# Two edits to a written order of work: a new list for one stretch, and four boundary columns moved

## The chip, the cores and the metric

The kernel runs on one core of a Trainium2 chip. Time is device time in microseconds (us), from the start of the program to its end; lower is better. Five engines work side by side, each taking its own instructions strictly in order: TensorE (PE, matmuls and transposes), VectorE (DVE), ScalarE (ACT), GpSimd (POOL) and SyncE (SP), which issues all DMA transfers. They wait for each other through semaphores. SBUF is the on-chip memory, PSUM the banks that PE writes to.

## The reference, cut to what matters

Input is x, 4 images of 256 x 256 positions with 64 channels, in 32-bit floats. Layer 0:

```python
h  = pw(layernorm(x, g1, b1), w_te, b_te)            # 64 -> 128 channels
F  = fft2(h)                                         # over the two image axes
fc = gelu(pw(concat(real(F), imag(F)), w_fc, b_fc))  # 256 -> 256 channels
sp = real(ifft2(re(fc) + 1j * im(fc)))
x1 = x + pw(sp, w_tp, b_tp)                          # 128 -> 64
h2 = pw(layernorm(x1, g2, b2), w_fe, b_fe)           # 64 -> 128
d  = gelu(depthwise_conv3x3(h2, w_dw) + b_dw)
x2 = x1 + pw(d, w_fp, b_fp)                          # 128 -> 64
```

Layer 1 takes x2 as a sequence along the first image axis, subtracts a moving average of 25, applies a complex matrix to each channel's first 128 frequencies, goes back and adds the average. The kernel makes one 256 x 256 matrix per channel of all this.

## The kernel before, in words

All Fourier transforms are matmuls with tables of sines and cosines, and symmetries halve them. Work comes in four kinds of units:

- **Forward chunks** (128 of them, 32 to an image): load a chunk of x ("fl"), its statistics ("fq" squares on ACT, line 327; "fr" sum on DVE, line 330; "fR", "fm" sum of squares, line 337; "fM" variance, line 341; "fp" power of -1/2 on POOL, line 347), scale it ("fx", POOL, line 354), then fold it by symmetry into halves ("fa", DVE, line 391), quarters ("fb", DVE, line 411) and halves again ("fh0", "fh1", POOL, line 416), transform along one axis ("y0", "y1", PE, line 422), evict ("yt0", "yt1", ACT, line 440) and store to DRAM. "fa" and "fh" write a tile xb that exists once; y0 and y1 read it. The squares go to a tile "sq" that also exists once and is shared by all statistics.
- **Pairs** of frequency columns (65 pairs to an image, two per period): transform along the other axis ("x", PE, line 527), evict ("xs", ACT, line 542), mix channels in two halves ("m0", "m1", PE, line 551), evict one part ("gc0", "gc1", ACT, line 565), add and subtract the other ("b0", "b1", DVE, line 570), gelu ("g0", "g1", ACT, line 574), fold ("p0", "p1", POOL, line 580), project ("z", PE, line 604), evict ("zs", ACT, line 612), transpose ("w", PE, line 621), evict ("zt", ACT, line 631).
- **Back steps**, one per period: transform back ("u", PE, line 653), evict ("us", ACT, line 670), combine ("uc", DVE, lines 683 and 684; "uf", DVE, lines 702 and 715) and store to DRAM.
- **Convolution chunks** (128, 32 to an image): load ("ul", "xl"), finish the first column ("c0", line 771), transform back along the first axis ("s", PE, line 813), add to x ("r0", "r1", DVE, lines 826 and 833), statistics of the same six kinds ("cq", "cr", "cR", "cm", "cM", "cp"), scale ("cx"), to channels ("t", "tt"), row sums ("T", POOL, lines 870 to 875), products ("gm", "gh", "em", "eh", PE, lines 896 and 915), evict and combine ("gc_", "cf", "ce", lines 935 to 947), edges ("cE"), gelu ("a", line 964), project ("o", PE, line 971), turn ("ft", PE, line 992), add and store ("st", line 1006).

Three frequency columns of each image that have no mirror partner among the stored ones are made apart, by "cc" (`other_columns`, line 773), once for each image, for its first chunk. It allocates the shared tile, loads two pieces into it, makes nine small DVE instructions on it and stores the result to DRAM; later chunks load it:

```python
v = shared.tile([P, 8, 2, C], F32, tag="sq", name=f"fix_{b}")
for i in range(2):
    nc.sync.dma_start(v[:, 2 * i : 2 * i + 2], u_ds[b][i][:, :, 0])   # line 781
...                                                # lines 784 to 796, DVE
nc.sync.dma_start(fixed[b], v[:, 3:6])             # line 797
```

The order is written out by hand. Program order is what the functions are called in, and each engine gets its instructions in that order; SP's alone are placed by the framework. The loop over periods n runs through a list of operations; each entry names an operation and an offset, and `do` first runs whatever the operation depends on by the table FOLLOWS:

```python
def period(n):
    for op, at in FULL if any(n - k in chunk_at for k in range(5)) else SPECTRUM:
        n0 = 2 * (n - S0) if op in PAIRS else n - S0 if op in BACK else n
        do(op, n0 + at)
```

For n below 35 a loop of its own (`starting`) does forward chunks beside layer 1's matrices. From n = 35 to 70 the list is SPECTRUM: forward chunks, pairs and back steps of the first image, and no convolution yet. From n = 71 on it is FULL, with convolution chunks. "cc" acts in the periods n = 71, 104, 136 and 169, the first convolution chunk of each image. Forward chunks end with n = 128, so the last two have none beside them. After the last period, layer 1 is applied in a stage of its own (line 1153), whose first inputs are loaded (lines 1133 and 1140) before the fourth image's chunks.

[...] a matmul into a bank waits for the last reader of what was there.

Of the kernel before, what the change touches and what calls it, by code (L numbers as in the profile page):

```python
# [129 lines left out]
def conv_seq_kernel(ctx: ExitStack, tc: tile.TileContext, a: dict, tables: bass.AP, out: bass.AP):  # L130
    nc = tc.nc
    x = a["x"]
# [11 lines left out]
    def column(ap):  # L144
        return ap.rearrange("(p o) -> p o", o=1)
# [46 lines left out]
    with tc.tile_pool(name="prep", bufs=1) as prep:  # L192

        def load(shape, name, src):
            t = prep.tile(shape, F32, tag=name, name=name)
            nc.sync.dma_start(t, src)
            return t

        w_te = load([C, HID], "w_te", a["w_te"])
        g1 = load([C, 1], "g1", column(a["g1"]))  # L200
        b1 = load([C, 1], "b1", column(a["b1"]))
# [1008 lines left out]
    def numbered(text):  # L1210

        return [(w.split(":")[0], int(w.split(":")[1]) if ":" in w else 0) for w in text.split()]

    follows = {}
    for line in FOLLOWS.replace("\n", "|").split("|"):
# [4 lines left out]

    FULL = numbered("""
        c0 s cf0:-3 cf1:-3 b0:-1 b1:-1 r0 r1 fx:-1 g0:-1 z:-2 zs:-2 x xs g1:-1 p0:-1 p1:-1
        o0:-4 fs0:-4 o1:-4 fs1:-4 ul:1 cq cr cR cm cM cp t0:-1 tt0:-1 t1:-1 tt1:-1 w:-2 zt:-2
        cx em:-3 eh:-3 T1:-1 T0:-1 fq fr fR fm fM fp m0 gc0 m1 gc1 ce0:-3 ce1:-3 cE:-3
        u us b0 b1 uc z:-1 zs:-1 x:1 xs:1 y0:-2 y1:-2 yt0:-2 yt1:-2 fl:1 a0:-3 a1:-3
        fa:-1 fb:-1 fh0:-1 fh1:-1 ft0:-4 ft1:-4 st0:-4 st1:-4 xl:1 cc w:-1 zt:-1 uf
        g0 g1 p0 p1 gm:-2 gh:-2 gc_0:-2 gc_1:-2 m0:1 gc0:1 m1:1 gc1:1 UL:1 XL:1
    """)

    SPECTRUM = numbered("""  # L1230
        fl:1 p0:-2 fq x z:-2 fr g0:-1 b1:-1 y0:-2 fx:-1 zs:-2 w:-2 fm xs g1:-1 m0 yt1:-2 zt:-2 fa:-1
        m1 u gc1 fR gc0 p0:-1 yt0:-2 fb:-1 us b1 fM p1:-1 b0 x:1 g1 fh1:-1 z:-1 fh0:-1 xs:1 m0:1
        zs:-1 uc gc0:1 w:-1 uf g0 m1:1 zt:-1 b0:1 fp y1:-1 gc1:1 p1
        UL:1 XL:1
    """)
    PAIRS = set("x xs m0 m1 gc0 gc1 b0 b1 g0 g1 p0 p1 z zs w zt".split())
# [119 lines left out]
```

## Time and profile before

| | |
|---|---|
| runs | 4531.76, 4535.45 and 4537.56 us (median 4535.45) |
| the profiled execution | 4535.69 us, span 4533.9 us |
| busy, share of the span | PE 96%, DVE 79%, POOL 61%, ACT 55% |
| chain that ended last | PE 75%, DVE 9%, POOL 4%, DMA 2%, issue 2% |

The profile is of one execution. Busy times are per engine; a group is all instructions of one line and shape, with total busy time, the mean of one in nanoseconds, and the idle time of the engine just before them. In the order of time, a line gives the start, the length, the engine, the source line, the operation, what it writes and reads, how many instructions were merged, and in brackets how long the engine had been idle and what released it. The clock column is TensorE's granted clock as a share of the full one.

### The profile page before, as it was taken

Reading aid. Unit: us, or ns where it says so; the run is one execution under the profiler, and the core shown is the slowest. Engines: PE = TensorE matmul, PEld = TensorE weight load, DVE = VectorE, ACT = ScalarE, POOL = GpSimd, SP = SyncE. Lnnn points to the kernel's source line nnn. Section 1 sums busy time; section 2 is a strip of 40 time slices with the busy share of each in tenths; the row PEclk is TensorE's granted clock in tenths of the full one; section 3 lists DMA queues with packets and bytes.
Section 4 is the critical chain, followed back from the end, with each engine's and each line's share of the span. In section 5 each row is a group of like instructions: output and inputs, shape, how many; then the busy total and the mean of one; then the engine's idle time right before and its main releaser. Section 6 shows DMA issues by size and latency. Waiting matters only on the chain.

```text
span 4533.9 us, 63718 instructions
## 1 busy us (share of the span) xinstructions
PE 4352.5 (96%) x22347; PEld 2231.7 (49%) x22347; DVE 3596.7 (79%) x5451; ACT 2505.2 (55%) x3686; POOL 2775.2 (61%) x1806
## 2 busy tenths in 40 slices
PE   7998888889999999999999999999999899999999
PEld 4543333345555555455555555555555455554444
DVE  6778999989999999999999777777777788862222
ACT  2337888666666666666666666666664344431111
POOL 5887888787888877788777555555554555530000
PEclk9999999999999999999999999999999999999999
DMA  5665555434444444444443333333334332329998
GB/s 171 203 191 153 141 143 149 136 107 131 131 130 131 134 130 133 125 134 135 136 137 119 93 117 98 98 105 97 105 105 131 111 103 93 102 78 321 324 331 268
DMA packets 764775, 655.02 MB, mean 144 GB/s; under 512 B 40141, under 2 KB 649375, under 8 KB 764328
## 3 DMA queue, kind: packets, MB, share of 16 engines
q1 hardware_dynamic: 764456, 650.95, 47.6%
q8 instruction: 179, 2.93, 0.3%
q14 instruction: 140, 1.15, 0.1%
HBM read 364.81 MB, written 286.00 MB: 144 GB/s over the span
## 4 chain that ended last, share of the span: by engine, by line
PE 75%; DVE 9%; POOL 4%; issue 2%; DMA 2%; SPq 0%; ACT 0%; POOLq 0%; DVEq 0%; ACTq 0%
PE ps_h_c L896 19%; PE ps_h_c L915 11%; PE ps_o L1153 8%; PE ps_p L551 7%; PE ps_f_c L971 5%; PE ps_s_c L813 5%; PE ps_z L604 4%; PE ps_u L653 4%; PE ps_x L527 4%; PE ps_t_c L850 3%; PE ps_ft_c L992 3%; DVE xb L391 2%; PE ps_y L422 2%; PE ps_zt L621 2%; DVE g L570 2%
## 5 line engine op out<-in xcount | busy, mean ns | idle before, releaser
L580 POOL TENSOR_TENSOR g<-g 128x512 f32<-128x512 f32 (+1 forms) x520 | 709.8, 1375 | 514.1 <-ACT g L574 514.0
L896 PE MATMUL ps_h_c<-td_c,wc_main 128*128 128x512 f32 x2048 | 923.9, 594 | 8.8 <-DVE h_c L941 8.8
L570 DVE TENSOR_TENSOR g<-ps_p,g 128x512 f32<-128x512 f32 x1040 | 693.6, 682 | 28.5 <-ACT g L565 10.4
L574 ACT ACTIVATE g<-g,b_fc 128x1024 f32<-128x1024 f32 (+1 forms) x520 | 585.7, 1146 | 225.7 <-DVE g L570 225.6
L347 POOL TENSOR_TENSOR rstd_c<-var_c,minus_half 128x16 f32<-128x16 f32 x128 | 371.8, 2905 | 478.7 <-DVE var_c L341 470.1
L551 PE MATMUL ps_p<-xs,wp 64*128 64x512 f32 (+1 forms) x2080 | 513.5, 604 | 63.9 <-ACT xs L542 61.7
L565 ACT COPY g<-ps_p 128x512 f32<-128x512 f32 (+1 forms) x520 | 299.1, 584 | 478.4 <-PE ps_p L551 476.4
L896 PEld LDWEIGHTS ps_h_c<-td_c,wc_main 128*128 128x128 f32 x2048 | 370.0, 191 | 379.1 <-issue 302.8
L915 PEld LDWEIGHTS ps_h_c<-td_c,wc_half 64*128 64x128 f32 x4032 | 418.0, 187 | 244.4 <-issue 195.0
L915 PE MATMUL ps_h_c<-td_c,wc_half 64*128 64x128 f32 (+1 forms) x4032 | 516.1, 393 | 3.9 <-POOL td_c L870 3.9
L1153 PE MATMUL ps_o<-xc,mt 128*128 128x512 f32 x1024 | 446.5, 598 | 15.7 <-DMA xc<-x_d 15.7
L347 POOL TENSOR_TENSOR rstd<-var,minus_half 128x16 f32<-128x16 f32 x128 | 373.0, 2914 | 82.0 <-DVE var L341 45.6
L416 POOL TENSOR_TENSOR xb<-xt 128x512 f32<-128x512 f32 x256 | 324.8, 1289 | 158.3 <-DVE xt L411 156.3
L947 DVE TENSOR_TENSOR h_c<-h_c,ps_h_c 128x512 f32<-128x512 f32 x512 | 317.4, 683 | 127.8 <-PE ps_h_c L915 127.7
L964 ACT ACTIVATE h_c<-h_c,b_conv 128x1024 f32<-128x1024 f32 x256 | 280.3, 1145 | 199.7 <-DVE h_c L960 199.7
L1167 DVE TENSOR_SCALAR oc<-ps_o,b_fp 128x512 f32<-128x512 f32 x128 | 96.1, 751 | 363.9 <-PE ps_o L1153 335.9
L940 DVE TENSOR_TENSOR h_c<-h_c,ps_h_c 128x512 f32<-128x512 f32 x256 | 175.8, 687 | 196.4 <-PE ps_h_c L915 192.8
L1153 PEld LDWEIGHTS ps_o<-xc,mt 128*128 128x128 f32 x1024 | 195.9, 192 | 265.6 <-issue 237.8
L527 PEld LDWEIGHTS ps_x<-tab,yb 128*64 128x64 f32 x4064 | 248.7, 139 | 146.6 <-issue 125.4
L604 PE MATMUL ps_z<-g,w_tp 128*64 128x512 f32 x1024 | 281.1, 610 | 38.9 <-POOL g L580 35.5
L551 PEld LDWEIGHTS ps_p<-xs,wp 64*128 64x128 f32 x2080 | 199.4, 188 | 212.8 <-issue 108.4
L1165 ACT ACTIVATE oc<-ps_o,b_fp 128x512 f32<-128x512 f32 x128 | 87.9, 687 | 375.5 <-PE ps_o L1153 326.8
(137 smaller groups left out, 7781.2 us busy)
## 6 DMA issues: line engine op xcount, KB each, us to landing
y_d<-yt SPq DMA_DIRECT2D x256, 256.0 KB, 2.6
yb<-y_d SPq DMA_DIRECT2D x256, 256.0 KB, 3.8
x_c<-in_x_dram SPq DMA_DIRECT2D x128, 512.0 KB, 5.3
u_d<-ut SPq DMA_DIRECT2D x256, 256.0 KB, 4.0
x_d<-st SPq DMA_DIRECT2D x128, 512.0 KB, 3.6
xc<-x_d SPq DMA_DIRECT2D x64, 1024.0 KB, 7.7
out_dram<-oc SPq DMA_DIRECT2D x256, 256.0 KB, 4.0
xt<-in_x_dram SPq DMA_DIRECT2D x504, 128.0 KB, 2.6
```

What stands on the lines that cost most here:

```text
L347: nc.gpsimd.tensor_tensor(rstd, var, minus_half.to_broadcast([P, n]), ALU.pow)
L416: nc.gpsimd.tensor_tensor(sums[j][:, i], x0, x1, (ALU.add, ALU.subtract)[i])
L527: nc.tensor.matmul(ps[r * C : (r + 1) * C, j * N + t * P : j * N + (t + 1) * P], blk[:, t, k, r * C : (r + 1) * C], tb[:, t, :], start=Tru ...
L551: nc.tensor.matmul(ps[:, :nf], wp[rows, cols], rhs[rows], start=True, stop=r == 1 or not pr["special"],)
L570: nc.vector.tensor_tensor(gt[:, i], re, gt[:, 1], op)
L574: nc.scalar.activation(g, g, AF.Gelu, bias=b_fc[:, half : half + 1])
L580: nc.gpsimd.tensor_tensor(g[:, 0], g[:, 0], g[:, 1], op)
L604: nc.tensor.matmul(ps[r * C : (r + 1) * C, :nf], w_tp, d[:, :nf], start=True, stop=True)
L896: nc.tensor.matmul(ps, wc_main[:, par, k, :], ts[(*j, k)].rearrange("p j i -> p (j i)"), start=True, stop=False,)
L915: nc.tensor.matmul(pss[k, par][:, s * P : (s + n) * P], wc_half[lo : lo + C, k, :], ts[(*at_q, k)][lo : lo + C, at : at + n, :].rearrange( ...
L947: nc.vector.tensor_tensor(g, g, m, (ALU.add, ALU.subtract)[r])
L1153: nc.tensor.matmul(ps[:, :nf], mts[i // CM][:, i % CM, t, to * P : (to + 1) * P], xc[:, t, :, :, i, :], start=t == 0, stop=t == 1,)
```

## The change

SPECTRUM is replaced by another order of the same operations with other offsets, and in FULL the entry "cc" moves from near the end of the list to just behind the statistics of the chunk, between "cM" and "cp". No operation is added or removed, except for what the offsets leave over from one period to the next.

```diff
     FULL = numbered("""
         c0 s cf0:-3 cf1:-3 b0:-1 b1:-1 r0 r1 fx:-1 g0:-1 z:-2 zs:-2 x xs g1:-1 p0:-1 p1:-1
-        o0:-4 fs0:-4 o1:-4 fs1:-4 ul:1 cq cr cR cm cM cp t0:-1 tt0:-1 t1:-1 tt1:-1 w:-2 zt:-2
+        o0:-4 fs0:-4 o1:-4 fs1:-4 ul:1 cq cr cR cm cM cc cp t0:-1 tt0:-1 t1:-1 tt1:-1 w:-2 zt:-2
         cx em:-3 eh:-3 T1:-1 T0:-1 fq fr fR fm fM fp m0 gc0 m1 gc1 ce0:-3 ce1:-3 cE:-3
         u us b0 b1 uc z:-1 zs:-1 x:1 xs:1 y0:-2 y1:-2 yt0:-2 yt1:-2 fl:1 a0:-3 a1:-3
-        fa:-1 fb:-1 fh0:-1 fh1:-1 ft0:-4 ft1:-4 st0:-4 st1:-4 xl:1 cc w:-1 zt:-1 uf
+        fa:-1 fb:-1 fh0:-1 fh1:-1 ft0:-4 ft1:-4 st0:-4 st1:-4 xl:1 w:-1 zt:-1 uf
         g0 g1 p0 p1 gm:-2 gh:-2 gc_0:-2 gc_1:-2 m0:1 gc0:1 m1:1 gc1:1 UL:1 XL:1
     """)
 
     SPECTRUM = numbered("""
-        fl:1 p0:-2 fq x z:-2 fr g0:-1 b1:-1 y0:-2 fx:-1 zs:-2 w:-2 fm xs g1:-1 m0 yt1:-2 zt:-2 fa:-1
-        m1 u gc1 fR gc0 p0:-1 yt0:-2 fb:-1 us b1 fM p1:-1 b0 x:1 g1 fh1:-1 z:-1 fh0:-1 xs:1 m0:1
-        zs:-1 uc gc0:1 w:-1 uf g0 m1:1 zt:-1 b0:1 fp y1:-1 gc1:1 p1
+        fr m0:-1 x g1:-1 xs p1:-1 gc0:-1 x:1 fq m0 z:-2 b0:-1 y1:-2 xs:1 fm gc0 m1 fR zs:-2 g0:-1
+        gc1 w:-2 fx:-1 fl:1 y0:-2 fM zt:-2 b0 p0:-1 fp z:-1 fa:-1 fb:-1 yt1:-2 fh1:-1 u b1 yt0:-2
+        zs:-1 us fh0:-1 uc m1:1 w:-1 g0 gc1:1 b1:1 p0 zt:-1 g1 p1 uf
         UL:1 XL:1
     """)
```

## The prediction

> **What bounds the kernel now.** I read the stretches first (busy time of each engine in windows that I cut at the stages), then the groups, the order in time and the waits inside them. Columns after the window: its length, then busy us and instructions of PE, PE weight loads, DVE, ACT and POOL.
>
> ```profile
> 416.00:823.00 407.00, 351.11 (x2208) 149.22 (x2208) 401.47 (x528) 328.48 (x498) 340.29 (x221) 1.00 0.52 145
> ...
> 1040.00:2484.00 1444.00, 1435.70 (x8222) 754.97 (x8220) 1365.60 (x2074) 956.06 (x1396) 1135.61 (x722) 1.00 0.44 132
> ...
> 2484.00:3423.00 939.00, 939.00 (x5468) 507.82 (x5466) 725.72 (x1170) 589.83 (x867) 500.54 (x361) 1.00 0.34 101
> ```
>
> 416 to 823 is the stretch without convolution (the list SPECTRUM): DVE is busy 401.5 of 407 us and PE 351.1, so DVE sets the pace. In the other two (the list FULL) PE is busy for 1435.7 of 1444 and all of 939 us: there each PE stall is lost time. In the order in time, line 683 returns every 14.68 us in the first stretch: 28 such periods and some irregular ones at both ends make up the list's 36. FULL's period is 27.73 us, later 26.01. DVE's groups in 416 to 823 (count | busy us, mean ns | idle before):
>
> ```profile
> L570 DVE TENSOR_TENSOR g<-ps_p,g 128x512 f32<-128x512 f32 x221 | 151.7, 686 | 3.9
> ...
> L391 DVE TENSOR_TENSOR xb<-xt 128x512 f32<-128x512 f32 x54 | 86.7, 1644 | 1.2
> ...
> L411 DVE TENSOR_TENSOR xt<-xb 128x512 f32<-128x512 f32 (+1 forms) x54 | 34.4, 678 | 0.0
> ```
>
> Lines 391 and 411 do the same arithmetic on the same size, but 391 takes 1644 ns and 411 678. The order in time (start, length) shows why:
>
> ```profile
> 511.10 1.29 POOL L580 TENSOR_TENSOR g<-g 128x512 f32<-128x512 f32 x1
> ...
> 511.41 3.21 DVE L391 TENSOR_TENSOR xb<-xt 128x512 f32<-128x512 f32 x2
> ...
> 512.74 1.33 POOL L580 TENSOR_TENSOR g<-g 128x512 f32<-128x512 f32 x1 [0.34 <-ACT g L574]
> ...
> 514.65 1.29 DVE L411 TENSOR_TENSOR xt<-xb 128x512 f32<-128x512 f32 x2
> ```
>
> Each of the two line-391 instructions ends only after a POOL addition. So of DVE's 14.68 us, 3.13 go to line 391 (start 511.41 to the next start 514.54) where line 411 needs 1.21: DVE's own sum is 14.68 - 1.9 = 12.8 us. PE needs 351.1/407 x 14.68 = 12.7, POOL 12.3, ACT 11.8. No list can do much better than 12.8.
>
> The second edit concerns "cc", nine small DVE instructions, four times in all. First time, in FULL's first period:
>
> ```profile
> 899.73 1.35 DVE L786 TENSOR_TENSOR fix<-fix 128x128 f32<-128x128 f32 x1
> ...
> 902.16 2.58 POOL L580 TENSOR_TENSOR g<-g 128x512 f32<-128x512 f32 x2
> ...
> 902.27 1.34 DVE L789 TENSOR_TENSOR fix<-fix 128x128 f32<-128x128 f32 x1
> ...
> 908.31 1.15 ACT L574 ACTIVATE g<-g,b_fc 128x1024 f32<-128x1024 f32 x1 [9.96 <-DVE g L570]
> ```
>
> They take 899.3 to 906.9, 7.6 us, stretched by POOL in the same way; ACT sits idle 9.96 us. The third time they take 1.8 us, with their loads issued 11 us ahead:
>
> ```profile
> 2675.31 1.23 SPq L781 DMA_DIRECT2D fix<-u_d  x2
> ...
> 2686.30 0.26 DVE L784 TENSOR_TENSOR fix<-fix 128x128 f32<-128x128 f32 x1
> ```
>
> The fourth waits for its loads, which SP issues behind four 1 MB loads of the last stage:
>
> ```profile
> 3496.03 13.50 SPq L1133 DMA_DIRECT2D xc<-x_d  x4
> ...
> 3513.66 2.66 SPq L781 DMA_DIRECT2D fix<-u_d  x2
> ...
> 3520.14 0.29 DVE L784 TENSOR_TENSOR fix<-fix 128x128 f32<-128x128 f32 x1 [14.52 <-DMA fix<-u_d]
> ...
> 3523.41 3.78 PE L896 MATMUL ps_h_c<-td_c,wc_main 128*128 128x512 f32 x4 [8.79 <-DVE h_c L941]
> ```
>
> Landing times in the DMA view (last column, us), and what PE does after a stall:
>
> ```profile
> fix<-u_d SPq DMA_DIRECT2D x8, 128.0 KB, 2.6
> ...
> fix_d<-fix SPq DMA_DIRECT2D x4, 192.0 KB, 3.1
> ...
> 1819.70 1.98 PE L604 MATMUL ps_z<-g,w_tp 128*64 128x512 f32 x4 [3.40 <-DVE h_c L941]
> ```
>
> Line 604 x4 takes 1.03 us at 1802.41 but 1.98 after the second cc's 3.40 us stall; the clock of 1816 to 1830 is 0.76.
>
> **What the Trainium skill says.** "SBUF — State Buffer", section "Who interferes with whom": a VectorE instruction with two SBUF inputs and a GpSimd instruction that reads SBUF exclude each other for a whole instruction. The trace agrees (1644 against 678 ns); lines 570 (one input in PSUM) and 330 (one input) keep 686 and 1208 ns beside POOL, and line 715 (two inputs) ran its 1.23 us at 505.31 under POOL's line 347, so that one hardly locks. "DMA: Bandwidth & Descriptors", section "Anatomy of one DMA — SWDGE (gpsimd) path": about 2 us of a DMA are fixed, mostly the receipt, and waiting is done on the issuing sequencer. Here 2.6 and 3.1 us. "TensorE: Matmul & The Clock Gate", section "What's actually happening": after about 3.4 us idle the clock halves. Agrees with the last line above.
>
> **The change, part 1: the list.** It adds and removes no instruction; it changes who queues behind whom. DVE's cycle becomes: fr, b0 of the odd pair, fm, fR, fM, b0 of the even pair, fa, fb, b1 even, uc, b1 odd, uf. Now fa, line 391, comes after POOL's p0 and beside its line 347 (fp), which hardly locks, so most of the 1.9 us goes. But new waits come. The longest loop of hand-overs, from the program's order, its buffers and banks, and the start-to-start times of the trace at 500 to 530, starting at ACT's xs (even) = 0:
> - m0 on PE after xs: 0.62 (503.68 to 504.30). PE in order: m0 1.06, z 0.90, y1 0.94, m1 1.03, w 0.59, then y0 at 5.14.
> - fa writes the only xb buffer, which y0 reads: from y0's start to DVE 1.15 (1002.43 to 1003.58): fa at 6.29. DVE, which ended b0 at 5.3, idles 1.0. POOL's p0 frees the port at about 6.3 too.
> - fa 1.30, fb 1.21, b1 even 1.33, uc 1.31: b1 odd at 11.44; the gelu g1 odd 1.45 later (501.18 to 502.63) at 12.89; it takes 1.05, then the next xs: 13.94.
>
> A second loop is as long: z even frees g for gc0 (1.15), zs and g0 follow on ACT (0.48 each), p0 1.24 later, then on POOL p0 1.3, fp 2.87, fh 2.52, p0 1.27, then uf holds the port 1.22, p1 1.35 to the next z: 13.9. Two loops at 13.9 that touch each other, with some twenty hand-overs: I take 14.1, between 13.9 and 14.7. At about 30 periods that is 30 x (14.68 - 14.1) = 17 us gained. At the seam to FULL the new list leaves one m, gc and y undone that the old had done: +2. Fill at the front: unknown, 0 ± 4.
>
> **Part 2: cc behind the statistics.** Line 780's tile is the one "sq" buffer. Before, cc's loads start after fm and DVE reaches the nine instructions at the period's end. Now they start after cm and DVE stands at them at once; behind them queue fr, fm, then cf_rest (947) or b (570); and fq on ACT waits until the result has left "sq" (line 797).
> - DVE: two loads, the second issued 0.65 after the first, land 2.6 later: 3.4 us. POOL's xn (354, 1.9 us) is running then (at 1800.28 in the second case), so the first instruction waits until about +5.0; then 1.9 us, since POOL waits for fM: +6.9.
> - First and second time: the store lands 2.6 after cc, fq 1.06, fm 1.2, fM: +12.2 where it was +2.6: 9.6 us late for everything behind, and on ACT gc, so PE's u and z stand about 8 us.
> - First time, outside the PE-bound part: before, the 7.6 us there; after, 9.6 earlier. fh, p and z come 10 late, the statistics of the next chunk 5: I take +4.
> - Second: PE stands 8 us and then runs 3 slow; before, it lost 4.1 (five periods from 1787.7 took 142.8 for 138.7). Less 1 of cover: +6.
> - Third: no forward chunk left, so no fq; but POOL's four td instructions (1.04 each) follow xn and let through one cc instruction each: cc ends near +10.9, line 947 8.5 late (2677.7 before), u waits for it 7.5 us, and the clock costs about 2; before, cc cost nothing (chunks at 26.01 on). +9.
> - Fourth: the loads stay behind the four big ones (until 3509.5) and land near 3516 to 3518; DVE now waits from 3501, with line 947 behind it, where before that ran at 3501.06. PE stops near 3504.5 until about 3519.5 and needs 10 us to where it stood at 3514.6: 3529.5 against 3523.4, some made good after: +5.
>
> Sum: +24 (12 to 34). If PE had work queued ahead of each wait it would be nothing; in FULL PE has no slack, so I take nothing off but what is said.
>
> **Sum.** -17 + 2 + 24 = +9 on the profiled execution's 4535.7 (span 4533.9, 1.8 around it), which is at the median of the runs, 4535.45: 4545. What counts as a change here is 0.2%, 9 us.
>
> **Rivals.**
> 1. *The list reaches DVE's floor and wins.* Place: the wait of fa for y0. If y0 came 1 us sooner (z not waiting for p1, m0 earlier), the period would be 12.9 to 13.3: 30 x 1.55 = 46 gained, -46 + 2 + 24 = -20: 4516. For: DVE's sum of 12.8. Against: the second loop at 13.9. It decides for faster below about 13.5 us a period.
> 2. *The list is no faster*: uf and p1 meet in the wrong order at the shared port, or hand-overs add 0.05 each, and the period is 14.6 or more. Nothing gained, +24 to +45: 4565. For: 14.68 has no hand-over on its path, since DVE never waits, while the new loops consist of them.
> 3. *cc is absorbed*: fix lands before POOL's xn starts, fq's wait is covered, each costs 1 to 3 us. Then -17 + 2 + 8 = -7, no change: 4529. For: in the FULL stretch before 2484 DVE has 5% free. Against: PE has none.
>
> **How the numbers follow.** As worked (net 0 to +20): 0.45, of which 0.17 under +9. Rival 2: 0.22. Rival 1: 0.16. Rival 3: 0.17, of which 0.03 beyond -9. So faster 0.19, same 0.31, slower 0.50. The likeliest case alone: 4536 to 4556. For 8 in 10, a tenth is left below (half of rival 1's cases) and a tenth above: 4519 to 4572.
>
> **What would show it.** Line 683's spacing near 14.1 (rival 1: 13.3; rival 2: 14.6 and over); line 391's mean down from 1644 to under 800 ns; DVE idle about 1 us before 391, released by PE's ps_y. DVE idle before line 784 released by DMA, 3 to 5 us three times and about 15 the fourth; ACT's line 327 waiting for the store of line 797; PE stalls of 7 to 9 us near the second and third cc. Past each cc the periods of 27.73, 26.01 and 16.37 should return unchanged. I am wrong if PE does not stall at cc or the new period is off by over 0.5.

## The result and the profile after

The changed kernel takes 4539.15 us (median of 6 runs, 4535.04 to 4542.61), the kernel before 4532.73 (6 runs, three of them those of the table above, 4528.77 to 4537.56): a ratio of 1.0012, interval 0.9999 to 1.0025. That is +6.4 us, inside the 9 us (0.2%) that the prediction took as no change; the interval just reaches below 1, so that these runs alone do not settle even its sign. Forecast were 4545, in a range of 4519 to 4572.

One caution for reading the traces. The profiled execution of the changed kernel took 4535.04 us and lies at the low end of its runs; that of before took 4535.69 and lies 3 us above its median. The pair of traces differs by -0.6 us in all, the medians by +6.4. So I read differences inside a stretch from the traces, and totals from the medians.

Behind the nearly unchanged time stand two opposite effects of over 20 us. First the stretches of the changed kernel, as shown for before (window: its length, then busy us and instructions of PE, PE weight loads, DVE, ACT, POOL, then the clock). I end the first window 23 us earlier, since the stretch ends earlier:

```profile
416.00:800.00 384.00, 356.70 (x2168) 142.61 (x2166) 363.08 (x524) 322.62 (x490) 359.74 (x218) 0.99 0.54 151
1040.00:2484.00 1444.00, 1431.48 (x8196) 752.12 (x8194) 1359.01 (x2065) 953.20 (x1392) 1131.08 (x717) 1.00 0.44 131
2484.00:3423.00 939.00, 933.39 (x5411) 504.06 (x5408) 724.00 (x1158) 587.77 (x862) 494.72 (x358) 1.00 0.34 100
```

In the stretch without convolution DVE is now busy 363.1 of 384 us; before, it was busy 401.5 of 407. In the two PE-bound windows PE is busy 4.2 and 5.6 us less than before: the second and the third cc lie in them.

DVE's groups of the first window (count | busy us, mean ns | idle before):

```profile
L570 DVE TENSOR_TENSOR g<-ps_p,g 128x512 f32<-128x512 f32 x218 | 149.4, 686 | 3.8
L391 DVE TENSOR_TENSOR xb<-xt 128x512 f32<-128x512 f32 x54 | 34.9, 688 | 13.8 <-PE ps_y L422 13.8
L411 DVE TENSOR_TENSOR xt<-xb 128x512 f32<-128x512 f32 (+1 forms) x54 | 34.4, 678 | 0.9
```

Line 391 fell from 1644 to 688 ns, which is line 411's speed: it no longer meets POOL's folds. In their place stands a wait for y0, 13.8 us in 27 times. One period in order of time:

```profile
512.33 0.56 ACT L542 COPY xs<-ps_x 128x512 f32<-128x512 f32 x1
...
517.31 1.28 POOL L580 TENSOR_TENSOR g<-g 128x512 f32<-128x512 f32 x1 [0.69 <-ACT g L574]
...
517.52 1.08 PE L422 MATMUL ps_y<-xb,tab 128*64 128x512 f32 x4
...
518.54 2.91 POOL L347 TENSOR_TENSOR rstd<-var,minus_half 128x16 f32<-128x16 f32 x1
...
518.71 1.29 DVE L391 TENSOR_TENSOR xb<-xt 128x512 f32<-128x512 f32 x2 [0.52 <-PE ps_y L422]
...
523.77 1.41 DVE L570 TENSOR_TENSOR g<-ps_p,g 128x512 f32<-128x512 f32 x2
...
526.27 0.56 ACT L542 COPY xs<-ps_x 128x512 f32<-128x512 f32 x1
```

From xs (line 542) to the xs of the next period it is 13.94 us. The prediction had y0 at 5.14 after xs (here 517.52 - 512.33 = 5.19), fa at 6.29 (6.38), b of the odd pair at 11.44 (11.44) and the next xs at 13.94 (13.94).

Now the first cc, in the same view:

```profile
866.41 1.23 SPq L781 DMA_DIRECT2D fix<-u_d  x2
...
869.59 0.29 DVE L784 TENSOR_TENSOR fix<-fix 128x128 f32<-128x128 f32 x1 [3.00 <-DMA fix<-u_d]
869.65 1.99 POOL L354 TENSOR_TENSOR xn_c<-x_c,rstd_c 128x1024 f32<-128x1024 f32 x1
869.80 1.99 DVE L785 TENSOR_TENSOR fix<-fix 128x128 f32<-128x128 f32 x1
...
873.20 0.34 SPq L797 DMA_DIRECT2D fix_d<-fix  x1
...
875.35 1.06 ACT L327 ACTIVATE sq<-xt 128x1024 f32<-128x1024 f32 x1 [10.07 <-DVE var L334]
...
876.93 3.68 PE L422 MATMUL ps_y<-xb,tab 128*64 128x512 f32 x8 [8.38 <-ACT g L565]
```

DVE stands 3.0 us for the loads, then a second time under POOL's line 354. ACT's line 327 begins 2.15 us after the store of line 797 was issued. The view names DVE's line 334 as its releaser, but that instruction had been done for 0.8 us (it began at 874.34 and took 0.18): what it really waited for was the shared tile "sq", which the store was still reading (a later run, below, names the store). Behind line 327 ACT's evictions queue, and PE idles 8.38 us. The second cc goes the same way:

```profile
1787.50 1.06 ACT L327 ACTIVATE sq<-xt 128x1024 f32<-128x1024 f32 x1 [9.77 <-DVE var L334]
...
1789.08 3.68 PE L653 MATMUL ps_u<-zt,tab 128*64 128x512 f32 x8 [7.16 <-ACT g L565]
```

The third cc, where line 354 and then the row sums (lines 870 to 875) run on POOL, and the clock of the window around it (the last number but two):

```profile
2663.56 0.29 DVE L784 TENSOR_TENSOR fix<-fix 128x128 f32<-128x128 f32 x1 [3.01 <-DMA fix<-u_d]
...
2665.68 1.12 DVE L786 TENSOR_TENSOR fix<-fix 128x128 f32<-128x128 f32 x1
...
2666.62 1.08 POOL L871 TENSOR_TENSOR td_c<-tt 128x512 f32<-128x512 f32 x1
...
2670.20 2.47 DVE L947 TENSOR_TENSOR h_c<-h_c,ps_h_c 128x512 f32<-128x512 f32 x4
...
2670.93 3.68 PE L653 MATMUL ps_u<-zt,tab 128*64 128x512 f32 x8 [5.61 <-DVE h_c L947]
...
2674.40 1.92 PE L604 MATMUL ps_z<-g,w_tp 128*64 128x512 f32 x4
```

```profile
2668.00:2680.00 12.00, 9.07 (x43) 4.65 (x44) 10.40 (x21) 3.54 (x5) 1.79 (x2) 0.72 0.14 43
```

The nine instructions take from 2663.56 to 2670.2. PE waits 5.61 us, and afterwards a line-653 and a line-604 group take 3.68 and 1.92 us, where they took 1.89 and 1.08 elsewhere in this trace: the clock is 0.72 in that window. The fourth stands behind the large loads as before, but now line 947 has to wait behind it too, and PE idles 15.83 us where it idled 8.79:

```profile
3489.76 13.67 SPq L1133 DMA_DIRECT2D xc<-x_d  x4
...
3503.53 4.14 SPq L781 DMA_DIRECT2D fix<-u_d  x2
...
3511.66 0.29 DVE L784 TENSOR_TENSOR fix<-fix 128x128 f32<-128x128 f32 x1 [16.96 <-DMA fix<-u_d]
...
3514.19 3.78 PE L896 MATMUL ps_h_c<-td_c,wc_main 128*128 128x512 f32 x4 [15.83 <-DVE h_c L947]
```

And what the tile of cc shows in total: DVE waited for its loads four times, where before it did once (14.5 us).

```profile
  DVE fix L784: 25.9, 4
...
DMA to landing us min/median/max: 1.9/2.5/7.7
```

### The profile page after: what moved, and what is told of

It reads as the page before. It is cut to its first block, busy times and chain, and to the rows that moved or that the text cites. A ratio compares the mean times of both kernels' runs of the same rounds, so it can differ in the third digit from the quotient of the medians.

```text
span 4533.3 us, 63491 instructions
## 1 busy us (share of the span) xinstructions
PE 4365.8 (96%) x22347; PEld 2223.1 (49%) x22347; DVE 3557.2 (78%) x5451; ACT 2505.6 (55%) x3686; POOL 2802.9 (62%) x1806
## 4 chain that ended last, share of the span: by engine, by line
PE 80%; POOL 7%; issue 4%; DVE 3%; DMA 3%; ACT 2%; SPq 0%; POOLq 0%; ACTq 0%; DVEq 0%
PE ps_h_c L896 19%; PE ps_h_c L915 11%; PE ps_o L1153 8%; PE ps_p L551 8%; PE ps_z L604 5%; PE ps_f_c L971 5%; PE ps_s_c L813 4%; PE ps_u L653 4%; PE ps_x L527 4%; PE ps_y L422 3%; POOL xb L416 3%; PE ps_ft_c L992 3%; PE ps_t_c L850 3%; POOL rstd L347 2%; PE ps_zt L621 2%
## 5 line engine op out<-in xcount | busy, mean ns | idle before, releaser
L580 POOL TENSOR_TENSOR g<-g 128x512 f32<-128x512 f32 (+1 forms) x520 | 737.2, 1430 | 531.6 <-ACT g L574 531.5
```

Of the source, the lines that this page charges most:

```text
L580: nc.gpsimd.tensor_tensor(g[:, 0], g[:, 0], g[:, 1], op)
```

## The experiments

To see where each kernel gains or loses, I set the start of the same instruction in its trace against that in the trace of before: line 683 up to the second image's cc, line 826 (convolution) after it. Negative is earlier than before. The step from one column to the next is what that place costs. (In the kernels that give cc a tile of its own, the line numbers from 784 on are 8 or 9 higher: the nine instructions begin at line 793, the store is line 805, and line 826 is line 834.)

| kernel | first line 683 | end of the stretch | past 1st cc | past 2nd | past 3rd | past 4th | median us |
|---|---|---|---|---|---|---|---|
| changed kernel | -4.1 | -25.3 | -18.5 | -14.9 | -6.3 | +0.3 | 4539.15 |
| new list alone | -4.2 | -25.4 | -23.7 | -25.8 | -25.8 | -25.8 | 4511.46 |
| cc moved alone | +5.6 | +3.9 | +9.0 | +12.7 | +21.5 | +29.8 | 4559.51 |
| own tile | -2.1 | -23.2 | -23.0 | -27.5 | -27.5 | -19.6 | 4516.38 (1 run) |
| loads ahead | -2.8 | -23.9 | -23.8 | -28.2 | -28.2 | -34.9 | 4502.02 |
| loads ahead, old place | -1.7 | -22.7 | -20.9 | -23.0 | -23.0 | -29.2 | 4505.97 |
| loads ahead, large loads later | -3.2 | -24.3 | -24.2 | -28.7 | -28.7 | -40.2 | 4495.09 |

The first column scatters by some 10 us: the kernel with cc moved alone, whose program up to there is that of before, stands at +5.6. Single executions differ by that much ahead of the stretch, so whether the new list also gains a few microseconds in its fill cannot be read here, and the readings below start from the first column.

**The two parts alone.** The new list with cc in its old place:

```diff
-        ... ul:1 cq cr cR cm cM cc cp t0:-1 ...        (FULL of the changed kernel)
+        ... ul:1 cq cr cR cm cM cp t0:-1 ...
-        ... st0:-4 st1:-4 xl:1 w:-1 zt:-1 uf
+        ... st0:-4 st1:-4 xl:1 cc w:-1 zt:-1 uf
```

> The new list alone, cc in its old place. Theory (the list gains about 25 us by the end of its stretch, and cc behind the statistics gives the same sum back): about 4533 - 24 = 4509, 4504 to 4514, ratio near 0.995; line 683 every 13.94 us in the stretch, the first cc as before (7.6 us on DVE beside POOL's folds). Rival (the lead made in the stretch cannot be kept, because the start of FULL waits for something else, so that cc's cost in the changed kernel is only the loss of that lead): between 4527 and 4533, and the lead of line 683 gone within the first five FULL periods.

Measured: 4511.46 us (before 4531.20), ratio 0.9955 (0.9942 to 0.9967): -19.7 us. The stretch gains 21.2 us in its 31 periods (-4.2 to -25.4). The seam to FULL takes 1.7 of it back, 2.1 more come at the second place, and the lead is kept to the end. The rival, that the lead is lost anyway, falls.

The other part, cc behind the statistics with the old SPECTRUM:

> cc behind the statistics alone, with the old list. Theory (cc costs +7, +3.5, +8.7 and +6.5 at its four places, whatever the list): about 4533 + 25 = 4558, 4552 to 4564, ratio near 1.0055; line 683 every 14.68 us in the stretch. Rival (the cost of the first cc is the price of the new list's seam, or the four overlap with the list's gain): 4533 + 15 to 19, about 4550, with the first cc costing 0 to 2.

Measured: 4559.51 us, ratio 1.0059 (1.0045 to 1.0073): +28.3 us. From the end of the stretch on, the four places cost 5.1, 3.7, 8.8 and 8.3, together 25.9; in the changed kernel they cost 6.8 (1.7 of it the list's seam), 3.6, 8.6 and 6.6. The first of these was expected at 7, which counted the seam in; the rival (about 4550, the first cc costing 0 to 2) falls. The parts add up within the scatter of the runs: -19.7 + 28.3 = +8.6, measured +6.4. In this trace the first cc's waits carry their right names (order in time):

```profile
896.26 1.94 DVE L784 TENSOR_TENSOR fix<-fix 128x128 f32<-128x128 f32 x1 [3.17 <-DMA fix<-u_d]
...
902.20 1.06 ACT L327 ACTIVATE sq<-xt 128x1024 f32<-128x1024 f32 x1 [10.10 <-DMA fix_d<-fix]
```

ACT's line 327 stood 10.1 us until cc's store had left the shared tile.

**Taking cc's waits away.** Two kernels take waits away by giving cc a tile of its own, with four columns (two kilobytes a partition); only its temporaries stay in "sq". The nine instructions keep their shapes; the first three change places. In the first the loads keep their place in the order, in the second an entry "cl" issues them at the end of the period before (at the end of both lists; the cut shows one).

```diff
+        def load_fix(j):                               # "cl"
+            v = fixes[b] = shared.tile([P, 4, 2, C], F32, tag="fix", ...)
+            for i in range(2):
+                nc.sync.dma_start(v[:, 2 * i : 2 * i + 2], u_ds[b][i][:, :, 0])
...
-            v = shared.tile([P, 8, 2, C], F32, tag="sq", name=f"fix_{b}")
+            v = fixes.pop(b)
+            q = shared.tile([P, 8, 2, C], F32, tag="sq", ...)   # temporaries alone
...
-            nc.sync.dma_start(fixed[b], v[:, 3:6])
+            nc.sync.dma_start(fixed[b], v[:, 1:4])
...
-        ... cq cr cR cm cM cc cp ...                   (changed kernel)
+        ... cq cr cR cm cM cl cc cp ...                (own tile)
+        ... cq cr cR cm cM cc cp ... UL:1 XL:1 cl:1    (loads ahead)
```

> The changed kernel with cc's four loaded columns and its result in a tile of their own, only the temporaries in the shared tile; the loads' place in the order is the changed kernel's. It tells the two waits apart: the squares of line 327 no longer wait for the store of the result to land, and the loads no longer wait for the shared tile, but are still issued beside the instructions that use them. If the loads go out 3 us before line 784's place at the latest (nothing but SP's own order holds them): the DVE wait of 3.0 us falls to 1 or nothing at the first three, and the costs fall nearly to those of the kernel with loads ahead; the fourth stays behind the four large loads, 15 us and more of wait. If they go out at the same time as now: DVE waits 3 us again, and only the 2 us of the store go, first and second 2 us cheaper each, third and fourth unchanged: about 4530.

Measured, in one run: 4516.38 us (before 4530.57). The loads went out early without any entry of the order being moved for it; the order in time at the first and the fourth cc:

```profile
859.88 0.56 SPq L781 DMA_DIRECT2D fix<-u_d  x1
...
868.68 0.28 DVE L793 TENSOR_TENSOR fixq<-fix 128x128 f32<-128x128 f32 x1
...
870.68 1.06 ACT L327 ACTIVATE sq<-xt 128x1024 f32<-128x1024 f32 x1 [3.22 <-issue]
...
3490.65 0.29 DVE L794 TENSOR_TENSOR fixq<-fix 128x128 f32<-128x128 f32 x1 [16.95 <-DMA fix<-u_d]
```

At the first, the later of the two loads is issued 8.8 us ahead of the nine instructions, DVE does not wait, and line 327 follows cc at once. The cost of the first three places is gone (+0.2 with the seam in it, -4.5 and 0.0 in the table). The fourth stays as it was (16.95 us, +7.9), since there the second of its loads waits in SP's queue and not for the tile. So at the first three it is the shared tile that makes cc dear behind the statistics: the loads can go only after line 337 has read the squares, and the next squares only after the store. Both waits went at once in this run, so it does not show what each costs alone at the first two; at the third, where no forward chunk's squares follow, the late loads and what they push under POOL's work make the whole cost.

> The changed kernel (new list, cc behind the statistics), but cc's two loads are issued at the end of the period before, into a tile of their own, and its temporaries alone lie in the shared tile; nine instructions of the same shapes, same result. Theory (what cc costs behind the statistics is the wait for its loads, 3.0 us three times and 17 the fourth, with the squares of line 327 held until the store of the result has landed): DVE does the nine in about 1.9 us beside POOL's line 347, no PE stall over 3 us near the first three, and the fourth loses its stall in the loads' queue too, which the kernel before has (8.8 us): 4533 - 25 - 6 (first cc, no longer stretched by POOL) - 3 (second) - 6 (fourth) = about 4493, 4486 to 4503. Rival (DVE has no room there, the nine instructions themselves push the statistics and line 947 late): 4515 to 4530, PE stalls of 4 us and more remain at the second and third.

Measured: 4502.02 us (before 4531.20), ratio 0.9933 (0.9921 to 0.9946). The first cc again:

```profile
867.90 0.29 DVE L793 TENSOR_TENSOR fixq<-fix 128x128 f32<-128x128 f32 x1
...
869.90 1.06 ACT L327 ACTIVATE sq<-xt 128x1024 f32<-128x1024 f32 x1 [3.22 <-issue]
...
871.48 1.94 PE L422 MATMUL ps_y<-xb,tab 128*64 128x512 f32 x8 [1.53 <-ACT g L565]
```

PE idles 1.53 us, where it idled 8.38. The nine instructions take 1.9 us each time, beside POOL's line 347. The fourth becomes a gain of 6.7, because its loads stand ahead of the large ones. The rival (the nine instructions themselves are too much there, 4515 to 4530) falls. It came out above the 4493 that I had named, though inside the range (4486 to 4503): against the new list alone the first cc gained 1.6, where I had counted 6, and the second 2.3, where I had counted 3; and for the list itself I had counted 25, where the trace of the list alone shows 21.6.

With the nine instructions in their old place and the loads ahead:

```diff
-        ... cq cr cR cm cM cc cp ...                   (loads ahead)
+        ... cq cr cR cm cM cp ...
+        ... st0:-4 st1:-4 xl:1 cc w:-1 zt:-1 uf
```

> As the last, loads issued ahead into a tile of its own, but with the nine instructions in their old place near the end of the period. Theory (the first cc is stretched to 7.6 us there by POOL's folds and the second stalls PE for about 4 us; only the fourth's wait for loads goes): 4509 - 6 = about 4503, 4497 to 4509. Rival (in the old place the fourth's wait was hidden as the chunks behind it have slack, or the stretch there costs nothing): 4509 as with the new list alone; or below the kernel with cc behind the statistics, if its place rather than its wait was the cost.

Measured: 4505.97 us, ratio 0.9943 (0.9931 to 0.9956); expected about 4503. Against the new list alone it gains at the fourth only (6.2 us). Against the place behind the statistics, the old place costs 1.7 us more at the first and 2.3 at the second. Without the waits, then, the place behind the statistics is the slightly better one; it was the waits that the changed kernel paid for.

**What is left at the fourth.** With loads ahead, PE still waited there, now for uc_c, whose load stands in SP's queue behind cc's store and the large loads (order in time):

```profile
3470.61 13.61 SPq L1142 DMA_DIRECT2D xc<-x_d  x4
...
3484.31 3.92 SPq L805 DMA_DIRECT2D fix_d<-fix  x1
...
3496.26 3.79 PE L821 MATMUL ps_s_c<-uc_c,tab 64*128 64x512 f32 x8 [5.22 <-DMA uc_c<-u_d]
```

```diff
-            mts = [matrix_load(seq, c) for c in range(0, CG, CM)]
-            xc = x2_load(seq, 0, 0, 1)
             for n in range(S0 + opened(B - 1) + 2, END):
                 period(n)
+                if n == S0 + opened(B - 1) + 5:
+                    mts = [matrix_load(seq, c) for c in range(0, CG, CM)]
+                    xc = x2_load(seq, 0, 0, 1)
```

> The kernel with loads ahead, and the first inputs of the last stage (mt and xc, lines 1148 on) loaded four periods later, after the third image's last and the fourth's first chunks, so that in the period of the fourth cc SP's queue holds no 13.6 us of large loads. With loads ahead PE still waited 5.2 us there for uc_c, whose load stands behind cc's store, which stands behind the large loads. Theory (SP's queue is what is left of the fourth's cost, about 7 us between the second and the third chunk): 4502 - 5 = 4497, 4492 to 4501. Rival (the large loads only move the same hold-up to a later period, where x_c and uc_c come late instead): 4500 to 4508.

Measured: 4495.09 us (before 4532.03), ratio 0.9918 (0.9904 to 0.9931), the fastest of all. At the fourth place the table shows -11.5 where loads ahead shows -6.7. What the edit did is not quite what I had planned, though. The loads moved four periods in the program, but SP's order is the framework's, and it still issued them here:

```profile
3474.14 0.33 SPq L805 DMA_DIRECT2D fix_d<-fix  x1
3474.57 4.01 SPq L1142 DMA_DIRECT2D xc<-x_d  x2
...
3483.80 1.94 SPq L1142 DMA_DIRECT2D xc<-x_d  x1
...
3490.52 1.99 PE L821 MATMUL ps_s_c<-uc_c,tab 64*128 64x512 f32 x8
```

The four large loads go out from 3474.57 to 3490.71, behind cc's store and with the chunks' own transfers between them, no longer four in a row; PE no longer waits for uc_c. So the gain belongs to that order in the queue; a load four periods later was not measured. Three chunks further the spacing of line 826 is that of before again (15.41, 16.70, then 16.37; before 15.40, 16.70, 16.38), so no hold-up comes back later.

**What holds the new list at 13.94.** Three runs on the kernel with loads ahead, one execution each:

```diff
-            xb = pool.tile([P, 2, 2, 2, WH, C], F32, tag="xb", ..., bufs=1)
+            xb = pool.tile([P, 2, 2, 2, WH, C], F32, tag="xb", ..., bufs=2)          # 1st, 3rd
-            gt = pool.tile([P, 2, 512], F32, tag=f"g{half}", ...)
+            gt = pool.tile([P, 2, 512], F32, tag=f"g{half}", ..., bufs=3 - half)     # 2nd, 3rd
-            x1s[j] = pool.tile([P, 2, W, C], F32, tag="x1", ..., bufs=6)
+            x1s[j] = pool.tile([P, 2, W, C], F32, tag="x1", ..., bufs=5)             # room, all
-            uc = ucs[j] = pool.tile([P, W, 2, C], F32, tag="uc", ...)
+            uc = ucs[j] = pool.tile([P, W, 2, C], F32, tag="uc", ..., bufs=1)        # room, 3rd
```

> On the kernel with loads ahead: the tile xb twice, so that fa (line 391) need not wait for y0's read of the chunk before; to make room, x1 five times rather than six, which the stretch without convolution does not touch. Read is the spacing of line 683 in that stretch, 13.94 us now. Prediction's account (two loops of hand-overs of the same length, one through y0 and fa, one through z, POOL's fp and fh, and p1): fa's wait of 0.5 us goes, the spacing stays at 13.9. Rival A (only the loop through y0 and fa binds): 13.4. Rival B (only the other binds): no change either, to be told apart by the third of these.

> On the kernel with loads ahead: the tile g of the first half three times, so that gc0 (line 565) need not wait for z, which frees some 0.3 us on ACT ahead of zs and g0; x1 five times. Prediction's account: the spacing stays at 13.9, since the loop through y0 and fa is untouched. Rival B (only the loop through z binds): 13.6. Rival A: 13.9 too.

> Both at once, xb twice and g of the first half three times; x1 five times and uc of the convolution once, which may cost time in the later stretch, so only the spacing in the first is read. Prediction's account (both loops bind): the spacing falls to about 13.6 only here. Rival A: 13.4 as with xb alone. Rival B: 13.6 as with g alone. Rival C (something else holds the period at 13.94, for example ACT's own order): 13.9 in all three.

Measured spacings of line 683: with xb twice 13.70 and 13.96 in turn (mean 13.83); with g three times 13.95; with both a pattern of five, 13.66, 14.98, 13.32, 15.00, 14.86 (mean 14.4). The first two agree with two equal loops (each freed alone brings 0.1 us or nothing). The third contradicts it: freed of both, the period got longer, which none of the four accounts had forecast. The groups of the stretch with xb twice, and then with both (count | busy us, mean ns):

```profile
L391 DVE TENSOR_TENSOR xb<-xt 128x512 f32<-128x512 f32 x54 | 39.2, 765 | 0.0
...
L715 DVE TENSOR_TENSOR ut<-ut,ut 128x1024 f32<-128x1024 f32 x14 | 24.6, 1755 | 0.0
```

```profile
L341 DVE SCALAR_TENSOR_TENSOR var<-var,squares 128x16 f32<-128x16 f32 x27 | 16.0, 591 | 0.9
```

Lines 391, 715 and 341 take 689, 1250 and 175 ns in the kernel with loads ahead. One place in the kernel with both, in order of time:

```profile
565.25 1.29 POOL L580 TENSOR_TENSOR g<-g 128x512 f32<-128x512 f32 x1
565.37 1.19 DVE L341 SCALAR_TENSOR_TENSOR var<-var,squares 128x16 f32<-128x16 f32 x1
```

A fold that starts 0.12 us before line 341 makes it 1.19 us instead of 0.17. It is the mutual exclusion that the Trainium skill, "SBUF — State Buffer", section "Who interferes with whom", describes for instructions of VectorE with two SBUF inputs and GpSimd. When a wait goes, DVE or POOL arrives earlier and meets the other there. Line 341 alone takes 0.42 us more in the mean, once a period, and the period is 0.42 longer; that fits, but other lines grew as well (lines 702 and 715 to 1414 and 1350 ns), and PE's clock in the stretch is 0.98, against 0.99 with loads ahead. How much each makes I did not separate. So what the three show is that a freed wait changes who meets whom at the shared port; what would hold the period without these meetings stays open. The single period of 13.3 stands among ones of 15.0, and no run shows that it could be kept. The three took 4513.65, 4524.64 and 4536.24 us (before 4534.05): in the fourth image's chunks the first fell from -38.7 to -22.2 against before, the others similarly, probably for the buffer that all three take from x1. So none of them is a candidate.

## Why the prediction was right, and where it was off

- **The list.** The mechanism was as said: line 391 leaves the folds (688 ns), and a loop of hand-overs through xs, y0, fa and b takes over, at the length worked out, 13.94. In the chain that the profile infers (470 to 540 us), three periods of five run through just these steps; two run through z, gc0, zs, g0, p0, fp and fh, the first part of the second loop, and then through the load of the next chunk, which the prediction had in no loop and no run varied. I then took 14.1 instead of the 13.94 and 13.9 of my own loops, to allow for hand-overs. This is the term that was mis-sized: 28 periods at 0.74 us make 20.7, measured 21.2 in the stretch, and I had 17. Two details inside it were off without changing its length: y0's weights have b0's read of the bank as a releaser too (0.17 us of idle; y0 came at 5.19 for 5.14), and DVE idles 0.5 us rather than 1.0, because line 334, 0.16 us before, takes 0.75 under POOL's line 354 and b0 ends later. The second loop is neither confirmed nor excluded: freeing g alone changed nothing.
- **The seam**: +2 expected, 1.7 shown by the new list alone.
- **cc on DVE.** A wait of 3.4 us for the loads (3.0 three times, 17.0 the fourth for "about 15"), then POOL's line 354. Line 784 slipped in ahead of it and line 785 was held instead; the end came at +6.8 for +6.9. At the third the nine ended at +9.9 for +10.9, with four of the nine meeting a row sum, as worked out.
- **cc's four prices**, in the changed kernel less the seam and with cc alone: first 5.1 and 5.1 (forecast 4), second 3.6 and 3.7 (6), third 8.6 and 8.8 (9), fourth 6.6 and 8.3 (5). Sum 23.9 and 25.9 (24). That the sum fits so well is in part luck: in the changed kernel the single prices miss by +1.1, -2.4, -0.4 and +1.6, which cancel. The second was mis-sized against before: PE's stall there was 7.16 us (8 expected). With the new list alone that place is 2.1 us better than before, though its cc is untouched; counted from there the second costs 5.7. The waits of PE there are no shorter with the list (3.42, 3.24 and 1.82 us; 3.40, 2.49 and 1.81 before), but the granted clock differs: 0.83, 0.91, 1.00 and 0.91 in four windows of 20 us from 1816 on before, 0.91, 0.91, 1.00 and 1.00 in those from 1792 on with the list. After the last wait twelve of line 527's matmuls take 1.91 us before and 1.04 with the list, and from that wait's end to the next line 896 it is 6.1 us before and 4.5 with the list, 1.6 of the 2.1. So most of it is TensorE's clock and not a shorter wait; why the clock fell in one trace and not in the other is open.
- **ACT's line 327 behind the store** was right in place and size (10.07 us of idle), and the kernel with its own tile shows that this and the held loads have one cause, the shared tile. The prediction had traced both waits to that tile; it did not say that they would go with it.
- **The base.** I summed on the profiled 4535.7, which lies 3 us above the median of before's six runs. Of the miss of 5.9 us this is 3.0; 2.6 is +9 forecast against +6.4, and the rest is rounding.
- **The rivals.** The list at DVE's floor (below 13.5) did not happen; the list without gain neither. cc absorbed gave -7 where +6.4 was measured, and the loss at its four places excludes it.

## What to carry to other kernels

When a small piece of work is moved, look first at the tile it borrows: with a tile that is shared with a stage on the path, its loads cannot run ahead and its store holds the next stage, and a move ahead by some ten microseconds turns a hidden transfer into a wait on two engines. A tile of its own (here two kilobytes a partition) and loads issued one period ahead turned +6.4 us into -29 (some 20 of it the new list's own), and breaking up the row of large loads in the same DMA queue brought 5 to 8 more. Two edits that come together are worth measuring apart when their forecast nearly cancels.

## What the runs showed that I had not expected

More buffers made a period longer: 13.94 us became 14.4 with xb and g both freed, and in it one of DVE's smallest instructions (128x16, 0.17 us), 0.12 us behind a POOL fold, took 1.19; whether that is all of it is not shown. And SP issued cc's loads 8.8 us early without any move in the order, once their tile was their own: it was the tile, not the place in the list, that had set when they started.
